# A spectral mixer with its filters: x turned on TensorE and a written-out order, in place of a channels-first copy of x, quarter-tile mixing and a planner

## The chip, the cores and the metric

One core of a Trainium2 chip runs the whole kernel. The metric is the device time of one execution in microseconds, the median of the runs shown.

## What is computed

The input x is 8 images of 128 x 128 positions with 96 channels, all float32. The layer has two halves:

```python
x = x + conv(_ln_c(x), ...)          # normalise over the channels, then the spectral mixer
t = t + ffn(_ln_t(t), ...)           # normalise again, then a quantised MLP 96 -> 384 -> 96

# conv:
x_pre = _soa(jnp.einsum('bhwc,mc->bhwm', x, w1), ...)       # 192 channels, scale * relu^2 + bias
xf = jnp.fft.rfft2(x_pre...)                                # over rows and columns
filt = ... # three small filters, resized to 128 x 65, complex
r = jax.nn.softmax(..., axis=1)                             # three weights per channel, from means over the image
comb = jnp.einsum('shwm,bsm->bhwm', filt, r)
xsp = jnp.fft.irfft2(xf * comb ...)
return jnp.einsum('bhwm,cm->bhwc', xsp, w2)                 # back to 96 channels
```

The MLP's products are of values rounded to fp8 (e5m2), its sums are rounded to float16.

## The kernel before

The Fourier transforms are products with cosine and sine matrices. Every image goes through three streams, which run interleaved: while one image is in the last, the next is in the second and the one after it in the first.

- **Stream a** (`before`, 32 units `u` of four columns of the image): x is read in blocks of 16 columns with rows on the partitions (`load_x`), only to measure mean and variance (`measure`, L581, VectorE). `rstd` makes the reciprocal deviations `ln_r` (ScalarE, VectorE, GpSimd). They go to memory (`store_r`, L650) and come back spread over 96 partitions (`load_r`, L654, tile `rB`). A second copy of x with the channels on the partitions, made by the host, is loaded too (`load_xT`, L646, tile `xT`). `scale` (L659, VectorE) multiplies both into `zT`, 96 x 512, and sums the channels. `project` (L672, TensorE) multiplies by `W1S`, `rectify` (L683) and `square` (L690) are ScalarE, `context` (L697) sums on GpSimd, `transform` (L701, TensorE) is the transform along the rows, `put` (L708, ScalarE) copies it out of PSUM and `store_y` (L711) writes it to the array `Yd`, from ScalarE's DMA queue.
- **Stream s** (`spectrum`, 33 groups `g` of spectrum rows): `load_y` and `load_t` (L842, L848) bring `yt` and the filter rows `tb`; `weigh` (L857) and `pack` (L866) are GpSimd; `along_w` (L874) is the transform along the columns and `filters_of` (L887) the filters' products, in four tiles of 64 x 64 of the array at a time, into `pf`. `make` and `times` (L913, L916, VectorE) multiply the spectra, `turn_back` and `real_basis` (L923, L938, L940, GpSimd) make `xf`. Two groups are then mixed at once by w2: channels 0 to 127 of each half are one product with `w2A` (`mix`, L995), the remaining 64 of each half go in 64 x 64 tiles with `w2B` (`mix_low`, L984), after four products of zeros that open the PSUM banks (L971). `mixed` (L1006) copies out, `invert` (L1011) is the inverse along the columns, `inverted` (L1018) copies out, `store_v` (L1021) writes `Vd`, from ScalarE's queue.
- **Stream c** (`after`, blocks of 16 columns, units of four): `last` (L1123, TensorE) is the inverse along the rows, `residual` (L1131, VectorE) adds x, `measure`, `rstd` and `quantise` (L1151) normalise into fp8 `z`, `turn` (L1156) transposes it by a product with an fp8 identity, `turned` (L1166) copies it out, `first` (L1170), `accumulated` (L1177), `biased` (L1181), `hidden` (L1185), `second` (L1192), `put` (L1203), `bias` (L1207) and `add_up` (L1210) are the MLP, `store` (L1213) writes the result.

**The order.** Nothing is issued where it stands in the code. Each operation is recorded by `at` with a written time: the start and length of its image's stream (`STREAMS`) plus an offset (`O`, for some images `OWN`). Beside the time, an operation carries the operations it needs (`after`), how many PSUM banks it takes and what frees them (`banks`, `until`). `in_order` takes the earliest operation whose needs are placed and for which a bank is free, moves what depends on it back by a lag, and so puts out one order with a bank for each tile. The order of instructions on SyncE, TensorE, VectorE, ScalarE and GpSimd is then fixed (`PINNED`). Six banks serve all products but the filters', which have two of their own (`psz`).

Of the kernel before, what the change touches and what calls it, by code (L numbers as in the profile page):

```python
# [22 lines left out]

# [21 lines left out]
MED = 192  # L45
# [12 lines left out]
NP = 16  # L58
WB = 16
HB = WB // 2  # L60
# [6 lines left out]
    "a": ((-2.3, 125.8), (125.5, 235.3), (361.7, 294.9), (654.8, 258.7), (914.4, 293.7), (1208.1, 250.0), (1549.9, 242.8), (1792.3, 246.3)),  # L67
    "s": ((145.6, 218.8), (374.7, 303.7), (677.8, 243.8), (924.7, 275.3), (1223.3, 298.2), (1520.9, 283.8), (1811.0, 258.1), (2086.7, 264.0)),
    "c": ((456.0, 260.1), (727.0, 260.5), (1018.6, 240.5), (1251.4, 323.7), (1604.0, 246.4), (1857.3, 253.2), (2101.5, 235.3), (2381.7, 138.0)),
# [3 lines left out]
    ("a", 0): {  # L73
        "a_load_xT": -1.97,
        "a_load_r": -5.06,
        "a_store_r": -9.58,
        "a_load_x": -10.466,
        "a_measure": -8.83,
        "a_scale": -1.29,
        "a_project_u0": 0.1,  # L80
        "a_rectify_u0": -4.22,
        "a_project_u2": 0.07,
        "a_rectify_u2": -5.38,
        "a_square": -3.56,
        "a_context": 0.88,
        "a_transform_u0": 1.37,
        "a_put_u0": 1.34,
        "a_transform_u2": 1.21,
        "a_put_u2": -5.7,
        "a_store_y": -2.773,  # L90
        "a_step": 0.26,
        "a_rstd": -4.27,
    },
    ("c", 6): {
        "c_step": 0.17,
        "c_rstd": 5.43,
        "c_quantise": 6.37,
        "c_first": 9.04,
        "c_accumulated": 8.29,
        "c_biased": 7.57,  # L100
        "c_load_v": 0.59,
        "c_last": 1.93,
        "c_residual": 1.66,
        "c_measure": -1.75,
        "c_turn": 8.21,
        "c_turned": 2.68,
        "c_hidden": 10.24,
        "c_second": 11.45,
        "c_put_blkq": 6.6,
        "c_bias": 8.21,  # L110
        "c_add_up": 7.54,
        "c_store": 8.05,
    },
    ("c", 7): {
        "c_step": 0.11,
        "c_rstd": 5.33,
        "c_quantise": 6.22,
        "c_first": 7.65,
        "c_accumulated": 2.03,
        "c_biased": 7.82,  # L120
        "c_load_v": -2.61,
        "c_last": 1.79,
        "c_residual": -0.5,
        "c_measure": -5.02,
        "c_turn": 6.63,
        "c_turned": 6.3,
        "c_hidden": 8.8,
        "c_second": 9.02,
        "c_put_blkq": 9.35,
        "c_bias": 3.04,  # L130
        "c_add_up": 9.99,
        "c_store": 3.47,
    },
    ("s", 7): {
        "s_load_y": -6.85,
        "s_load_t": -3.503,
        "s_weigh": -2.2,
        "s_pack": -2.89,
        "s_along_w_g1": -1.69,
        "s_copy_sr": -3.98,  # L140
        "s_along_w_g0": -5.22,
        "s_filters_of": -1.38,
        "s_make_dmALUsubtract": -2.12,
        "s_make_dpALUadd": -2.45,
        "s_times_t1dm00": -7.26,
        "s_times_t2dp10": -11.08,
        "s_times_t3dm01": -3.94,
        "s_times_t4dp11": -1.04,
        "s_turn_back_g0": -0.01,
        "s_turn_back_g1": -0.53,  # L150
        "s_real_basis_g0": 0.5,
        "s_real_basis_g1": -13.48,
        "s_along_w_g0_x": -1.76,
        "s_alone_z": -4.41,
        "s_filters_of_x": -1.0,
        "s_alone_t": -3.96,
        "s_alone_x": -1.27,
        "s_mix_low": 0.05,
        "s_mix": -0.12,
        "s_mixed": -3.05,  # L160
        "s_invert": 0.88,
        "s_inverted": -2.36,
        "s_store_v": -9.843,
    },
}

T_WEIGHTS, T_CONST, T_ROWS = -112.0, -48.0, (-19.0, 94.0)

O = {
    "a_load_xT": -3.37,  # L170
    "a_load_r": -8.87,
    "a_store_r": -11.4,
    "a_load_x": -10.636,
    "a_measure": -7.71,
    "a_scale": -0.88,
    "a_project_u0": -0.28,
    "a_rectify_u0": -6.09,
    "a_project_u2": 0.13,
    "a_rectify_u2": -4.67,
    "a_square": 0.25,  # L180
    "a_context": 0.82,
    "a_transform_u0": 1.31,
    "a_put_u0": -2.63,
    "a_transform_u2": 1.05,
    "a_put_u2": -2.74,
    "a_store_y": -5.993,
    "s_load_y": -4.81,
    "s_load_t": -2.653,
    "s_weigh": -0.53,
    "s_pack": -0.19,  # L190
    "s_along_w_g1": 0.49,
    "s_copy_sr": -4.8,
    "s_along_w_g0": 0.64,
    "s_filters_of": 0.97,
    "s_make_dmALUsubtract": 0.87,
    "s_make_dpALUadd": 0.85,
    "s_times_t1dm00": -3.01,
    "s_times_t2dp10": -9.29,
    "s_times_t3dm01": -2.33,
    "s_times_t4dp11": 1.37,  # L200
    "s_turn_back_g0": 1.79,
    "s_turn_back_g1": 2.03,
    "s_real_basis_g0": 2.18,
    "s_real_basis_g1": -7.56,
    "s_along_w_g0_x": 0.15,
    "s_alone_z": -4.37,
    "s_filters_of_x": 1.5,
    "s_alone_t": -0.23,
    "s_alone_x": -3.9,
    "s_mix_low": 1.23,  # L210
    "s_mix": 1.38,
    "s_mixed": -0.75,
    "s_invert": 2.22,
    "s_inverted": 0.88,
    "s_store_v": -1.203,
    "a_step": 0.53,
    "a_rstd": -3.83,
    "c_step": 0.22,
    "c_rstd": 4.21,
    "c_quantise": 5.11,  # L220
    "c_first": 6.59,
    "c_accumulated": 5.43,
    "c_biased": 7.0,
    "c_load_v": -2.91,
    "c_last": 0.76,
    "c_residual": -1.01,
    "c_measure": 0.49,
    "c_turn": 6.04,
    "c_turned": 3.07,
    "c_hidden": 7.86,  # L230
    "c_second": 8.37,
    "c_put_blkq": 5.18,
    "c_bias": 3.81,
    "c_add_up": 8.94,
    "c_store": 3.77,
}
BANKS = 6

LAG, TRANSFER_LAG = 0.15, 2.28
PINNED = (  # L240
    mybir.EngineType.SP,
# [26 lines left out]
def _columns(p, r):  # L268

    if p < NP - 1:  # L270
        return [(g, cs) for g in (2 * p, 2 * p + 1) for cs in range(2)]
    return [(NG - 1, 0), (NG - 1, 1)] + [(NG, 0), (NG, 1)] * (r == 0) + [(NG + 1, 0)]


def _constants():
# [14 lines left out]

    turned = []
    for p in range(NP):
        for r in range(2):
            for g, cs in _columns(p, r):
                k = g + 1 + 32 * r if g < NG else 32 if g == NG else 64 * r
                turned.append(k + 64 * cs)
# [4 lines left out]
        "GK": np.concatenate([cos, -sin[1:-1]])[turned] * norm,  # L301
# [18 lines left out]
Op = namedtuple("Op", "time seq what args key needs banks until")  # L320


def in_order(ops):


    keys = {op.key for op in ops}
    assert len(keys) == len(ops)
    left, then, ready, held = {}, defaultdict(list), [], []
    place = {op.key: op.time for op in ops}
    for op in ops:  # L330
        needs = {k for k in op.needs if k in keys}
        left[op.key] = len(needs)
        for k in needs:
            then[k].append(op)
        if not needs:
            heappush(ready, (op.time, op.seq, op))

    free, banks, frees, order = list(range(BANKS)), {}, defaultdict(list), []
    for op in ops:
        for u in op.until:  # L340
            frees[u].append(op)
    pending = {op.key: list(op.until) for op in ops}
    while len(order) < len(ops):
        entry = heappop(ready)
        op = entry[-1]
        if op.banks > len(free):
            held.append(entry)
            continue
        banks[op.key], free = free[: op.banks], free[op.banks :]
        order.append((op, tuple(banks[op.key])))  # L350
        for follower in then[op.key]:
            lag = TRANSFER_LAG if follower.key[1].startswith(("load", "store")) else LAG
            place[follower.key] = max(place[follower.key], place[op.key] + lag)
            left[follower.key] -= 1
            if not left[follower.key]:
                heappush(ready, (place[follower.key], follower.seq, follower))
        for taker in frees[op.key]:

            if len(taker.until) == taker.banks:
                free.append(banks[taker.key][taker.until.index(op.key)])  # L360
            else:
                pending[taker.key].remove(op.key)
                if not pending[taker.key]:
                    free += banks[taker.key]
        while held:
            heappush(ready, held.pop())
    return order


@with_exitstack  # L370
def metaformer_kernel(ctx: ExitStack, tc: tile.TileContext, a: dict, out: bass.AP):
    nc = tc.nc
    x, xT = a["x"], a["xT"]

# [960 lines left out]
```

## Time and profile before

| | before |
|---|---|
| median of 3 runs (lowest to highest) | 2754.84 us (2751.38 to 2756.22) |
| profiled execution: time, span | 2756.22 us, 2754.4 us |
| mean granted TensorE clock | 0.97 |
| DMA | 618.05 MB, 224 GB/s, 480,023 packets |
| largest TensorE lines (recorded) | L672 519 us, L701 431 us, L874 532 us in two groups |
| largest lines of the others | L923 POOL 520 us, L1151 ACT 461 us, L1177 ACT 456 us, L1181 DVE 428 us |

A group of instructions is shown as line, engine, operation, output<-inputs and their sizes, with its busy time and the mean time of one. A float32 product counts as two matmul instructions. A matmul's recorded end is modelled and overlaps the start of the next, so recorded times of a line are longer than what the line takes from its engine; the distance from start to start is the latter. In the slices each digit is the busy share of a fortieth of the span.

### The profile page before, as it was taken

How to read it: one execution, taken by the hardware profiler on the slowest of the kernel's cores; microseconds unless marked ns; L12 is line 12 of the kernel's file. 1: busy time of each engine (PE TensorE's matmuls, PEld its weight loads, DVE VectorE, ACT ScalarE, POOL GpSimd, SP SyncE). 2: the span in 40 equal slices, each digit the busy share in tenths (PEclk: the TensorE clock that was granted, in tenths of full speed). 3: DMA queues.
4: the chain of work that ended last, by engine and by line, in shares of the span. 5: the costliest groups of instructions: out<-in, count | busy, mean ns of one | idle time of the engine just before them, and what ended most of it. 6: DMA issues, size and time to landing. Idle time of an engine off the chain costs nothing.

```text
span 2754.4 us, 69406 instructions
## 1 busy us (share of the span) xinstructions
PE 2567.8 (93%) x25130; PEld 1953.0 (71%) x25130; DVE 2276.1 (83%) x5887; ACT 2233.0 (81%) x4452; POOL 2122.2 (77%) x3246
## 2 busy tenths in 40 slices
PE   4989999999999999999999999999999998999765
PEld 2668877777677777777677777777777776677433
DVE  3557667798898999889898889889889878999786
ACT  2665556699888879889998878889988997888898
POOL 1239997888788878988688969888788886889432
PEclk9899999999999999999999999999999998999896
DMA  7888777977688866878687757888777774656441
GB/s 205 263 263 253 242 224 241 287 233 251 209 255 260 252 213 196 271 242 262 220 258 245 243 171 220 273 259 257 231 239 242 230 222 147 185 178 190 149 129 62
DMA packets 480023, 618.05 MB, mean 224 GB/s; under 512 B 174542, under 2 KB 381270, under 8 KB 479658
## 3 DMA queue, kind: packets, MB, share of 16 engines
q1 hardware_dynamic: 424386, 462.60, 56.8%
q10 hardware_dynamic: 55296, 151.02, 14.7%
q8 instruction: 199, 3.26, 0.5%
q14 instruction: 142, 1.16, 0.1%
HBM read 405.36 MB, written 208.16 MB: 223 GB/s over the span
## 4 chain that ended last, share of the span: by engine, by line
PE 68%; DVE 13%; ACT 7%; POOL 4%; DMA 4%; issue 3%; SPq 1%; POOLq 0%; ACTq 0%; DVEq 0%
PE px L672 13%; PE pz L874 10%; PE py L701 10%; PE pv L995 7%; PE pf L887 6%; PE pg L1011 5%; PE ph L1170 4%; PE pk L1123 4%; PE po L1192 3%; PE pv L984 3%; DVE t L916 3%; DVE y L1181 2%; ACT h L1185 2%; ACT y L1177 2%; DVE st L581 2%
## 5 line engine op out<-in xcount | busy, mean ns | idle before, releaser
L923 POOL TENSOR_TENSOR rr<-t,t 128x390 f32<-128x390 f32 x512 | 520.4, 1017 | 60.4 <-DVE t L916 60.0
L672 PE MATMUL px<-W1S,zT 97*128 97x240 f32 x2048 | 519.4, 379 | 34.1 <-DVE zT L659 29.2
L1177 ACT CAST y<-ph 128x512 f16<-128x512 f32 x768 | 456.0, 603 | 24.2 <-PE ph L1170 22.4
L672 PEld LDWEIGHTS px<-W1S,zT 97*128 97x128 f32 x2048 | 377.2, 194 | 130.0 <-issue 33.7
L1151 ACT ACTIVATE z<-t,ln_m,ln_r 128x96 fp8e5<-128x96 f32 x960 | 461.2, 492 | 8.6 <-POOL ln_m L614 5.7
L1181 DVE TENSOR_SCALAR y<-y,b1q 128x512 f16<-128x512 f16 x768 | 427.5, 568 | 28.2 <-ACT y L1177 25.6
L683 ACT ACTIVATE rl<-px 128x480 f32<-128x480 f32 x512 | 295.7, 581 | 177.5 <-PE px L672 160.2
L701 PE MATMUL py<-X,F 128*128 128x384 f32 x1024 | 430.7, 507 | 2.1 <-ACT X L690 1.9
L1185 ACT ACTIVATE h<-y 128x1536 fp8e5<-128x1536 f16 x256 | 386.2, 1509 | 2.2 <-DVE y L1181 1.6
L659 DVE SCALAR_TENSOR_TENSOR zT<-xT,rB 96x512 f32<-96x512 f32 x256 | 339.8, 1328 | 53.1 <-DMA rB<-Rd 26.5
L874 PEld LDWEIGHTS pz<-F,yt 128*128 128x128 f32 x2080 | 301.4, 192 | 72.0 <-DVE t L1131 5.9
L1210 POOL TENSOR_TENSOR t<-t,o 128x1536 f32<-128x1536 f32 x64 | 210.1, 3282 | 167.8 <-DVE o L1207 165.8
L874 PE MATMUL pz<-F,yt 128*128 128x130 f32 x2080 | 329.0, 281 | 10.2 <-DVE t L1131 4.7
L857 POOL TENSOR_TENSOR tb<-tb,r 128x384 f32<-128x384 f32 (+1 forms) x264 | 287.0, 1087 | 59.7 <-DVE r L808 23.1
L916 DVE TENSOR_TENSOR t<-dm,pf 128x390 f32<-128x390 f32 x512 | 282.6, 552 | 43.8 <-PE pf L887 18.4
L1170 PE MATMUL ph<-zT,W1q 96*128 96x512 fp8e5 x768 | 293.5, 397 | 19.1 <-DVE zT L1166 13.9
L708 ACT COPY yst<-py 128x384 f32<-128x384 f32 x512 | 246.4, 486 | 74.3 <-PE py L701 67.8
L916 DVE TENSOR_TENSOR t<-dp,pf 128x390 f32<-128x390 f32 x512 | 280.3, 548 | 0.0
L940 POOL TENSOR_TENSOR xf<-rr 128x378 f32<-128x378 f32 x256 | 255.3, 997 | 19.7
L995 PEld LDWEIGHTS pv<-w2A,xf 128*128 128x128 f32 x2048 | 246.8, 194 | 13.6 <-issue 1.5
L995 PE MATMUL pv<-w2A,xf 128*128 128x96 f32 x2048 | 255.2, 278 | 0.0
L938 POOL TENSOR_TENSOR xf<-rr 128x390 f32<-128x390 f32 x256 | 250.1, 977 | 0.0
(126 smaller groups left out, 5210.5 us busy)
## 6 DMA issues: line engine op xcount, KB each, us to landing
Yd<-yst ACTq DMA_DIRECT2D x256, 384.0 KB
yt<-Yd SPq DMA_DIRECT2D x256, 384.0 KB
xb<-in_x SPq DMA_DIRECT2D x64, 768.0 KB
xT<-in_xT SPq DMA_DIRECT2D x128, 384.0 KB
rB<-Rd SPq DMA_DIRECT2D x128, 384.0 KB
tb<-T SPq DMA_DIRECT2D x256, 192.0 KB
Vd<-gst ACTq DMA_DIRECT2D x128, 384.0 KB
xr<-in_x SPq DMA_DIRECT2D x64, 768.0 KB
```

Of the source, the lines that this page charges most:

```text
L659: nc.vector.scalar_tensor_tensor(zTs[(b * NU + u) % NZT][:C, :, :], kept["xT", hb][:, :, w].rearrange("c h w -> c w h"), 1.0, kept["rB", h ...
L672: nc.tensor.matmul(px[:, i * (MED + SCTX) : (i + 1) * (MED + SCTX)], lhsT=zTs[(b * NU + u) % NZT][:, i0 + i, :], rhs=W1S, start=True, stop ...
L701: nc.tensor.matmul(py, lhsT=F1, rhs=kept["X", u][:, i0 : i0 + 2, :].rearrange("h w m -> h (w m)"), start=True, stop=True)
L874: nc.tensor.matmul(pz[:, u * 2 * L : (u + 1) * 2 * L], lhsT=y, rhs=F2[:, cs, :], start=True, stop=True)
L916: nc.vector.tensor_tensor(work(name, g), kept[d, g], pair(g, sign, c), ALU.mult)
L923: nc.gpsimd.tensor_tensor(kept["rr", g][:, :, 2 * i : 2 * i + 2, :], kept[ta, g], kept[tb, g][:, :, ::-1, :], op)
L995: nc.tensor.matmul(kept["pv", p, r][:, i * C : (i + 1) * C], lhsT=kept["xf", g][:, cs, r, :], rhs=w2A, start=False, stop=(i == len(_column ...
L1151: nc.scalar.activation(z, t, AF.Identity, bias=m, scale=r, saturate=False)
L1170: nc.tensor.matmul(kept["ph", u, n], lhsT=W1q[:, n * 128 : (n + 1) * 128], rhs=kept["zT", u], start=True, stop=True)
L1177: nc.scalar.copy(kept["y", u][:, n, :], kept.pop(("ph", u, n)))
L1181: nc.vector.tensor_scalar(y, y, b1q[:, n : n + 1], 0.0, ALU.add, ALU.max)
L1185: nc.scalar.activation(kept["h8", u], kept["y", u], AF.Copy, saturate=False)
```

## The change

Stream a no longer has a channels-first copy of x. The x block that was read for measuring is scaled in place, with rows on the partitions (`scale`, VectorE); four transposes a unit (`turn`, TensorE) put it channels first in PSUM, and `turned` (ScalarE) copies it to `zT` and sums it. The round trip of the deviations through memory goes, and with it `xT`, `rB` and `Rd`. The copies of y are stored two units at a time, from SyncE's queue instead of ScalarE's, and so is `Vd`.

Stream s mixes by single groups, not pairs. The quarter tiles and the zeros go: `w2B` is padded with zeros to 128 rows x 192 columns, and the 64 remaining channels of both halves are one product with it, on which the two products with `w2A` add up. `xf` has three buffers instead of four, `xb` three instead of two.

The planner `in_order` goes, with all `after`, `banks` and `until`. The operations are sorted by their written time alone, and the six PSUM banks are taken in turn. SyncE is no longer among the `PINNED` engines. The written times are others: from the third image on each stream takes 335 an image. `filters_of` is the same in both.

```diff
 STREAMS = {
-    "a": ((-2.3, 125.8), (125.5, 235.3), (361.7, 294.9), (654.8, 258.7), (914.4, 293.7), (1208.1, 250.0), (1549.9, 242.8), (1792.3, 246.3)),
-    "s": ((145.6, 218.8), (374.7, 303.7), (677.8, 243.8), (924.7, 275.3), (1223.3, 298.2), (1520.9, 283.8), (1811.0, 258.1), (2086.7, 264.0)),
-    "c": ((456.0, 260.1), (727.0, 260.5), (1018.6, 240.5), (1251.4, 323.7), (1604.0, 246.4), (1857.3, 253.2), (2101.5, 235.3), (2381.7, 138.0)),
+    "a": ((0, 118), (119.0, 243.0), (361.0, 335), (695, 335), (1030, 335), (1365, 335), (1700, 335), (2035, 335)),
+    "s": ((141, 242.1), (412, 335), (747, 335), (1082, 335), (1417, 335), (1752, 335), (2087, 335), (2430, 240)),
+    "c": ((465, 335), (800, 335), (1135, 335), (1470, 335), (1805, 335), (2140, 335), (2475, 240), (2715, 150)),
 }
...
 PINNED = (
-    mybir.EngineType.SP,
     mybir.EngineType.PE,
...
-def in_order(ops):
...
-    stream, free_banks = [None], []
+    events = []
...
-    ps = ctx.enter_context(tc.tile_pool(name="ps", bufs=1, space=PSUM))
+    ps = ctx.enter_context(tc.tile_pool(name="ps", bufs=6, space=PSUM))
...
-    def at(time, what, *args, after=(), banks=0, until=(), name=None):
-        name = name or what.__name__
-        ops.append(Op(time, len(ops), what, args, (stream[0], name) + args, after, banks, until))
+    def at(time, what, *args):
+        events.append((time, len(events), what, args, stream[0]))
...
-        t = ps.tile([128, 512], F32, name=name, tag=f"bank{free_banks.pop(0)}")
+        t = ps.tile([128, 512], F32, name=name, tag="ps")
...
-    w2B = const.tile([128, C], F32, name="w2B")
+    w2B = const.tile([128, 2, C], F32, name="w2B")
...
         def others():
+            nc.gpsimd.memset(w2B, 0.0)
             for i in range(2):
-                nc.sync.dma_start(out=w2B[64 * i : 64 * i + 64, :], in_=a["w2T"][128:, :])
-            make_identity(nc, ident)
+                nc.sync.dma_start(out=w2B[64 * i : 64 * i + 64, i, :], in_=a["w2T"][128:, :])
...
+            xb = pa.tile([128, WB, C], F32, name="xb", tag="xb", bufs=3)
...
-        def load_xT(hb):
-            t = kept["xT", hb] = pa.tile([C, H, HB], F32, name="xT", tag="xT")
-            nc.sync.dma_start(out=t, in_=xT[b, hb, :, :, :])
-
-        def store_r(blk):
-            t = kept["Rd", blk] = dram.tile([2, H, HB], F32, name="Rd", tag="Rd")
-            nc.sync.dma_start(out=t.rearrange("f h w -> h f w"), in_=kept["r", blk].rearrange("h (f w) -> h f w", f=2))
-
-        def load_r(hb):
-            t = kept["rB", hb] = pa.tile([C, H, HB], F32, name="rB", tag="rB")
-            nc.sync.dma_start(out=t, in_=kept["Rd", hb // 2][hb % 2].partition_broadcast(C))
-
-        def scale(u):
-            hb, q = divmod(u, 2)
+        def scale(blk, q):
             w = slice(q * QW, (q + 1) * QW)
-            nc.vector.scalar_tensor_tensor(
-                zTs[(b * NU + u) % NZT][:C, :, :],
-                kept["xT", hb][:, :, w].rearrange("c h w -> c w h"),
-                1.0,
-                kept["rB", hb][:, :, w].rearrange("c h w -> c w h"),
-                ALU.mult,
-                ALU.mult,
+            xb = kept["x", blk]
+            r = kept["r", blk][:, w].unsqueeze(2).to_broadcast([128, QW, C])
+            nc.vector.tensor_tensor(xb[:, w, :], xb[:, w, :], r, ALU.mult)
+
+        def turn(u):
+            blk, q = divmod(u, NQ)
+            pz = kept["pz"] = bank("pzt")
+            for i in range(QW):
+                nc.tensor.transpose(pz[:C, i * 128 : (i + 1) * 128], kept["x", blk][:, q * QW + i, :], ident)
+
+        def turned(u):
+            nc.scalar.activation(
+                zTs[u % NZT][:C, :, :].rearrange("c w h -> c (w h)"),
+                kept["pz"][:C, :],
+                AF.Copy,
                 accum_out=kept["gacc"][:, u : u + 1],
             )
 
         def project(u, i0):
-            px = kept["px", u, i0] = bank("px")[:, : 2 * (MED + SCTX)]
...
         def put(u, i0):
-            if ("yst", u) not in kept:
-                kept["yst", u] = pa.tile([128, QW, MED], F32, name="yst", tag="yst", bufs=3)
-            nc.scalar.copy(kept["yst", u][:, i0 : i0 + 2, :].rearrange("j w m -> j (w m)"), kept.pop(("py", u, i0)))
+            if u % 2 == 0 and i0 == 0:
+                kept["yst"] = pa.tile([128, 2 * QW, MED], F32, name="yst", tag="yst")
+            w0 = u % 2 * QW + i0
+            nc.scalar.copy(kept["yst"][:, w0 : w0 + 2, :].rearrange("j w m -> j (w m)"), kept["py", i0])
 
         def store_y(u):
-            nc.scalar.dma_start(out=Y[b][:, u * QW : (u + 1) * QW, :], in_=kept.pop(("yst", u)))
+            w0 = (u - 1) * QW
+            nc.sync.dma_start(out=Y[b][:, w0 : w0 + 2 * QW, :], in_=kept["yst"])
...
-        def mix_low(p):
...
-                    nc.tensor.matmul(
-                        kept["pv", p, r][half, :n],
-                        lhsT=zeros[rows, :64],
-                        rhs=zeros[rows, :1].to_broadcast([64, n]),
-                        start=True,
-                        stop=False,
-                    )
-            for i in range(5):
-                for h in range(2):
-                    for r in range(2):
-                        if i < len(_columns(p, r)):
-                            g, cs = _columns(p, r)[i]
-                            half, rows = slice(64 * h, 64 * h + 64), slice(64 * r, 64 * r + 64)
-                            nc.tensor.matmul(
-                                kept["pv", p, r][half, i * C : (i + 1) * C],
-                                lhsT=kept["xf", g][rows, cs, 2, half],
-                                rhs=w2B[rows, :],
-                                start=False,
-                                stop=False,
-                            )
...
+        def mix(g):
+
+            xf = kept.pop(("xf", g))
+            pv = kept["pv"] = bank("pv")[:, : 4 * C]
+            for cs in range(2 if g <= NG else 1):
+                o = pv[:, cs * 2 * C : (cs + 1) * 2 * C]
+                nc.tensor.matmul(o, lhsT=xf[:, cs, 2, :], rhs=w2B.rearrange("m n c -> m (n c)"), start=True, stop=False)
+                for u in range(2):
+                    nc.tensor.matmul(
+                        o[:, u * C : (u + 1) * C], lhsT=xf[:, cs, u, :], rhs=w2A, start=False, stop=(u == 1)
+                    )
...
+        def store_v(g):
+            nc.sync.dma_start(
+                out=V[b][:, 4 * (g - 1) : 4 * (g + 1), :],
+                in_=kept["gst"].rearrange("w g (j c) -> w (g j) c", c=C),
             )
             kept_v[b] += 1
 
...
     stream[0] = None
-    at(t - 3 * length / NU - 5, next_pool, after=[(None, "weights")])
-    for op, banks in in_order(ops):
-        free_banks[:] = banks
-        op.what(*op.args)
+    at(t - 3 * length / NU - 5, next_pool)
+    events.sort(key=lambda e: e[:2])
+    for _, _, what, args, _ in events:
+        what(*args)
...
```

## Prediction

> **What bounds the kernel now.** I read the busy shares first, then the slices, then a steady stretch, then the starts inside that stretch.
>
> ```profile
> PE 2567.8 (93%) x25130; PEld 1953.0 (71%) x25130; DVE 2276.1 (83%) x5887; ACT 2233.0 (81%) x4452; POOL 2122.2 (77%) x3246
> PE   4989999999999999999999999999999998999765
> PE 68%; DVE 13%; ACT 7%; POOL 4%; DMA 4%; issue 3%; SPq 1%; POOLq 0%; ACTq 0%; DVEq 0%
> ```
>
> PE is busy nearly everywhere but in the first slices and the last three, and holds two thirds of the chain of waits. The steady stretch, 600 to 2100 us (columns: PE, PEld, DVE, ACT, POOL busy):
>
> ```profile
> 600.00:2100.00 1500.00, 1466.05 (x14727) 1129.97 (x14726) 1328.45 (x3411) 1317.31 (x2666) 1262.67 (x1899) 0.99 0.77 240
> ```
>
> The groups of lines of that stretch count 1208 px matmuls of 256 an image, so 4.72 images pass: **318 us an image**. A matmul's recorded end overlaps its successor, so busy PE overstates; the timeline's start-to-start distances don't:
>
> ```profile
> 1305.69 0.39 PE L1156 MATMUL pz<-ident,z 128*96 128x128 fp8e5 x4
> 1306.01 0.36 PE L971 MATMUL pv<-zeros 64*64 64x384 bf16 x4
> 1306.19 0.83 PE L984 MATMUL pv<-w2B,xf 64*64 64x96 f32 x32
> 1306.95 1.08 PE L672 MATMUL px<-W1S,zT 97*128 97x240 f32 x4
> 1307.87 1.92 PE L995 MATMUL pv<-w2A,xf 128*128 128x96 f32 x16
> 1309.63 0.64 PE L874 MATMUL pz<-F,yt 128*128 128x130 f32 x4
> ```
>
> zeros take 0.18 us from start to next start, the 32 quarter-tile instructions of w2B 0.76, the 16 of w2A 1.76 (1.82 in another set; I use 1.79). Read alike between 1300 and 1345 us: px x4 0.81, py x2 0.65, pz x6 0.67, pf x24 0.83, pg x2 0.70, pk x2 0.66, ph 0.22, po x12 0.51, the fp8 turn x4 0.23 to 0.32 (0.25 taken). Times their numbers in an image: px 64 x 0.81 = 51.8, py 41.6, pz 43.6, pf 27.0, zeros and w2B 15.0, w2A 28.6, pg 22.4, pk 21.1, ph 21.1, po 16.3, turn 8.0, together 296.5 us. So PE really works **93%** of the 318 us; 21.5 us are slack. ACT (1317 us) and DVE (1328) are each at 88% of this stretch, POOL at 84%.
>
> **The skill.** "TensorE: Matmul & The Clock Gate", Terms, gives a transpose mode that is "4× faster for FP32"; no transpose-mode matmul runs in the kernel before, so its trace is silent. The same page, LDWEIGHTS, has a load time go with columns, P/1.2: about 80 ns for 96 and 107 for 128. Here 16 fp32 loads of w2A's 128 columns take 1.96 us, 122 ns each: somewhat more. "Perfetto Trace Analysis", Identifying the Most-Contended Engine, calls matmul busy a bad metric; 1466 busy against some 1395 from starts agrees. "SBUF — State Buffer", SBUF: two separate sides, has a DVE op with two SBUF inputs and a GpSimd op that reads SBUF lock each other out. The scaling at L659 spreads from 985 to 3882 ns (median 1170), which fits.
>
> **Part by part, PE.** Each unit of four columns gains four fp32 transposes (1024 in all), stationary the x tile of 96 columns, moving the 128-column identity. If the mode costs one pass, the nearest row is the fp8 turn of the same shape, 0.23 us per four. If loads don't hide, the row of its loads sets it (0.46 per four):
>
> ```profile
> 1305.46 0.46 PEld L1156 LDWEIGHTS <-z 128*96 128x96 fp8e5 x4
> ```
>
> I take 0.30 per four: 32 x 0.30 = **9.6 us an image** (7.4 to 14.7). If it cost a plain fp32 product, three 130-column pz products in 0.67 us give 0.22 each, and 128 of them 28 us. That is a rival below.
>
> Mixing: per pair of groups 4 zeros, 32 quarter instructions and 16 of w2A go (0.18 + 0.76 + 1.79 = 2.73, x 16 = 43.7 us an image). In come 65 sets of one 192-column and two 96-column fp32 products. By columns a set is 0.32 + 2 x 0.16 = 0.64 us (384 columns take 0.65); by six loads of 122 ns it is 0.73, which I take: 47.5. **+3.8 us** (from -2 to +6, the upper end where the w2A products keep their 0.22). The filters' own 64x64 tiles are the same in both. PE work: 296.5 + 9.6 + 3.8 = **310 us an image**.
>
> **The others.** DVE loses L659 (340 + 20 us for its accumulator reads) and gains 256 products of 128x384; the nearest row, L1131, takes 550 ns, and as both inputs are in SBUF I allow 740: 141 to 190 us. Net -170 to -220, about -25 us an image. It buys nothing while PE sets the period. ACT gains 256 evacuations of 96x512: the fp16 evacuation of 512 columns takes 603 ns, with an accumulator read of DVE's 79 about 0.69, +177 us or 22 an image: 279 + 22 = 301. It stays under PE's 310 but leaves less room. The 384 stores, 326 ns each on ACT's queue, move to SP: up to 15.6 us an image back to ACT's sequencer. POOL: nothing of size, the rows of L923 and L857 stay.
>
> SP loses 128 loads of xT, 128 of rB, 64 stores of Rd and gains 128 merged Y stores and 128 V stores: some 1030 issues at 0.36 us instead of 1100. But a store on SP waits for its copy, and the loads behind it wait too: x, Yd and T loads, and then pack, weigh and PE. Written leads are 11 us (T) to 80 us (x); I price this at zero as long as a store waits less than that, else the order rival applies. DMA loses 100 of 618 MB; at 0.77 busy this is cover, not gain. At the start it saves the Rd round trip (DMA Rd, rB and xT hold 17% of the chain's first 300 us), but the first matmul is at 42.8 us and the next stage is PE work: zero, up to -30.
>
> Order: the planner, which knows what each operation waits for and which bank is free, goes. The new order sorts hand-written times, with six PSUM banks taken in turn; PE is in order, so each wrong place is idle PE. The trace can't show this. Bounds: the planner's 93%, or 85% (a 365 us period). I take 91.5%: 310 / 0.915 = **339 us**.
>
> **Sum.** After: first products near 40 us (before 42.8); stage a of image 0, 51.8 + 41.6 + 9.6 = 103 us of PE, at 95% 108; then a of image 1 with s of image 0, 103 + 140.5 = 243.5, at 95% 256; then the written 104 us until c of image 0 starts: 508, say 510 (before: first pk at 495). Six periods to c of image 6: 2034. The written tail, 2912 - 2475 = 437, stretched by 5% (in the trace the c streams stretch 7.6%: pk from 495 to 2713 where 462 to 2523 is written): 459. Last block and close: 12. Together 3015. The profiled execution's time is 1.8 us above its span of 2754.4, and the median 2754.84 lies between; so the prediction is **3015 us**, +9.4%.
>
> **Rivals.**
> 1. *Hidden, not slower.* The added 13.4 us fit into the 21.5 us of slack, and DVE, 25 us lighter, refills pz and pf banks sooner. Period 318, time 2755. It decides where PE's idle at the changed order can fall below 2.5% of the period. For: L1131 and L913 are rows where DVE and PE wait on each other (DVE dp waited 66 us for pz). Against: 93% is reached with a planner, the new order has none, and ACT gets heavier.
> 2. *Transposes at full fp32 price.* +18.6 us an image: 329 / 0.915 = 359; six periods 120 more and the edges 40: 3175. Against: the skill's mode.
> 3. *The order costs more.* PE at 86%: 360 us, 3015 + 126 + 20 = 3160. For: PE and ACT both near 90% leave little room to absorb misplaced work, and stores block SP.
> 4. *The order costs nothing.* 93%, 333 us, the tail unstretched, the start quicker: 2930.
>
> **Numbers.** Forecast 0.52; rival 4 and a little below it 0.17; rival 3 0.15; rival 2 0.10; rival 1 0.06 (0.03 beyond 0.2% faster, 0.02 within, the rest just slower). 0.2%, 5.5 us, is about what measuring can tell from no change. The range takes in rival 4's value and nearly rival 3's: 2910 to 3155; 0.2 lies outside.
>
> **What would show it.** Right: transposes of 128x128 fp32 in one instruction each, four starting within 0.3 us; px units 335 to 345 us apart per image; PE's slices still 9 from the fourth on; DVE's share near 68%, ACT's near 80%; POOL and DVE idle longer on PE rows. Wrong: 2048 instead of 1024 transpose instructions (rival 2); SP waiting on ACT's yst or gst with PE idle on tb, yt or xb DMAs, or large PE idle behind ACT's PSUM copies (rival 3); a period of 318 (rival 1). The forecast falls if PE's start-to-start work isn't near 310 us an image, or PE's share of the steady stretch isn't 90 to 93%.

## The result, and the profile after

The changed kernel takes **2852.83 us** (2849.47 to 2855.48, four runs) against 2753.11 for the kernel before: ratio 1.0361, 95% interval 1.0343 to 1.0379. It is slower, as forecast, but by 3.6% and not 9.4%; 2853 lies below the range's 2910. The profiled execution took 2855.48 us, its span is 2853.7.

The page of the changed kernel: busy shares, TensorE's slices, the chain of waits by engine.

```profile
PE 2696.3 (94%) x22618; PEld 2109.1 (74%) x22618; DVE 2130.0 (75%) x5630; ACT 2358.3 (83%) x4972; POOL 2024.5 (71%) x3255
PE   6999999999999999999999999999999998988765
PE 78%; DVE 9%; ACT 6%; POOL 3%; issue 2%; DMA 1%; SPq 0%; POOLq 0%; DVEq 0%; ACTq 0%
```

TensorE's busy time is 128 us longer, and its share of the chain rises from 68% to 78%: the changed kernel is more clearly TensorE's than the one before. VectorE lost 146 us, GpSimd 98, ScalarE gained 125. The steady stretch from 600 to 2100 us (columns PE, PEld, DVE, ACT, POOL busy, clock, DMA share, GB/s):

```profile
600.00:2100.00 1500.00, 1491.17 (x12959) 1188.02 (x12958) 1203.44 (x3182) 1350.13 (x2894) 1168.65 (x1864) 1.00 0.60 194
```

The px matmuls of the same stretch, in the kernel before and in the changed one:

```profile
L672 PE MATMUL px<-W1S,zT 97*128 97x240 f32 x1208 | 303.8, 373 | 6.1 <-DVE zT L659 3.3 <-ACT y L1177 1.9 <-ACT gst L1018 0.4
L551 PE MATMUL px<-W1S,zT 97*128 97x240 f32 x1176 | 291.7, 370 | 0.0
```

1176 of 256 an image are 4.59 images: **326.5 us an image**, where the kernel before took 318. One cycle of the timeline of TensorE there:

```profile
1310.22 0.58 PE L811 MATMUL pv<-w2A,xf 128*128 128x96 f32 x4
1310.64 0.52 PE L809 MATMUL pv<-w2B,xf 128*128 128x192 f32 x2
1310.99 0.58 PE L811 MATMUL pv<-w2A,xf 128*128 128x96 f32 x4
1311.41 1.00 PE L551 MATMUL px<-W1S,zT 97*128 97x240 f32 x4
1312.25 0.38 PE L944 MATMUL ph<-zT,W1q 96*128 96x512 fp8e5 x1
1312.47 0.67 PE L966 MATMUL po<-W2q,h 128*128 128x96 fp8e5 x12
1312.98 0.60 PE L538 MATMUL pzt<-ident,xb 128*96 128x128 f32 x4
1313.51 0.90 PE L729 MATMUL pf<-RW,tb 52*64 52x130 f32 x24
```

From start to start, four transposes take 0.53 us here and 0.44 to 0.48 in the cycles after it; the mean over the stretch is 0.46. A set of the padded mixing takes 0.76. With the other rows as before, TensorE's work is 296.5 us, plus 32 x 0.46 = 14.7 for the transposes, plus 65 x 0.76 - 43.7 = 5.7 for the mixing: 317 us an image. So it works **97%** of the 326.5 us, against 93% before. The work grew by 20.5 us an image and the image by 8.6: some 12 us of it fell into time in which TensorE had been idle.

The whole profile can be cut at the first pk product of image 0 and of image 6, as the prediction's sum was:

| us | to c of image 0 | six periods | from there to the end | span |
|---|---|---|---|---|
| before | 495 | 1860 | 400 | 2754 |
| forecast | 510 | 2034 | 471 | 3015 |
| after | 495 | 1941 | 418 | 2854 |

The forecast is 15, 93 and 53 us too long in the three parts.

### The profile page after: what moved, and what is told of

The parts are those of the page before. It is cut to its first block, busy times and chain, and to the rows that moved or that the text cites. A ratio compares the mean times of both kernels' runs of the same rounds, so it can differ in the third digit from the quotient of the medians.

```text
span 2853.7 us, 63672 instructions
## 1 busy us (share of the span) xinstructions
PE 2696.3 (94%) x22618; PEld 2109.1 (74%) x22618; DVE 2130.0 (75%) x5630; ACT 2358.3 (83%) x4972; POOL 2024.5 (71%) x3255
## 4 chain that ended last, share of the span: by engine, by line
PE 78%; DVE 9%; ACT 6%; POOL 3%; issue 2%; DMA 1%; SPq 0%; POOLq 0%; DVEq 0%; ACTq 0%
PE px L551 15%; PE py L576 11%; PE pz L716 10%; PE pv L811 7%; PE pf L729 7%; PE pv L809 6%; PE pg L832 5%; PE ph L944 5%; PE pk L900 4%; PE pzt L538 4%; PE po L966 3%; DVE y L955 2%; DVE t L759 2%; ACT y L951 2%; ACT h L959 2%
## 5 line engine op out<-in xcount | busy, mean ns | idle before, releaser
L955 DVE TENSOR_SCALAR y<-y,b1q 128x512 f16<-128x512 f16 x768 | 417.1, 552 | 255.9 <-ACT y L951 254.0
L551 PEld LDWEIGHTS px<-W1S,zT 97*128 97x128 f32 x2048 | 369.9, 191 | 100.0 <-ACT zT L541 23.9
L959 ACT ACTIVATE h<-y 128x1536 fp8e5<-128x1536 f16 x256 | 381.7, 1491 | 26.8 <-DVE y L955 26.8
L811 PE MATMUL pv<-w2A,xf 128*128 128x96 f32 x2080 | 305.6, 270 | 0.0
L811 PEld LDWEIGHTS pv<-w2A,xf 128*128 128x128 f32 x2080 | 303.4, 193 | 0.0
L984 POOL TENSOR_TENSOR t<-t,o 128x1536 f32<-128x1536 f32 x64 | 198.7, 3105 | 108.1 <-DVE o L981 108.1
L809 PE MATMUL pv<-w2B,xf 128*128 128x192 f32 x1040 | 267.4, 339 | 3.9 <-POOL xf L781 3.7
L779 POOL TENSOR_TENSOR xf<-rr 128x390 f32<-128x390 f32 x256 | 232.2, 907 | 15.8
L729 PE MATMUL pf<-RW,tb 52*64 52x130 f32 x6240 | 239.8, 282 | 1.7 <-POOL rr L766 1.7
```

The source lines that it names most:

```text
L551: nc.tensor.matmul(px[:, i * (MED + SCTX) : (i + 1) * (MED + SCTX)], lhsT=zTs[u % NZT][:, i0 + i, :], rhs=W1S, start=True, stop=True,)
L729: nc.tensor.matmul(pf[64 * h : 64 * h + 64, s, u * 2 * L : (u + 1) * 2 * L], lhsT=tb[p, m0 : m0 + 64], rhs=RW[p, :], start=True, stop=True,)
L809: nc.tensor.matmul(o, lhsT=xf[:, cs, 2, :], rhs=w2B.rearrange("m n c -> m (n c)"), start=True, stop=False)
L811: nc.tensor.matmul(o[:, u * C : (u + 1) * C], lhsT=xf[:, cs, u, :], rhs=w2A, start=False, stop=(u == 1))
L955: nc.vector.tensor_scalar(y, y, b1q[:, n : n + 1], 0.0, ALU.add, ALU.max)
L959: nc.scalar.activation(kept["h8", u], kept["y", u], AF.Copy, saturate=False)
```

## The experiments

All runs are compared with the kernel before on the same chip; the medians of the kernel before were 2750 to 2755 us. Theory P says that TensorE's work sets the time and the written order keeps it at work; what the rivals say stands with each run. The "steady stretch" is always 600 to 2100 us of the run's profile; its px matmuls, 256 an image, give the time of an image.

**1. Without the transposes.** From the changed kernel:

```diff
-                nc.tensor.transpose(pz[:C, i * 128 : (i + 1) * 128], kept["x", blk][:, q * QW + i, :], ident)
...
-                kept["pz"][:C, :],
+                kept["x", blk][:C, :, :].rearrange("c w h -> c (w h)")[:, lo : lo + QW * 128],
```

> The changed kernel (2853 us) without its 1024 transposes on TensorE: ScalarE copies as many elements to zT straight from the x block in SBUF, so the projection works on unturned numbers; ScalarE's and VectorE's work stays. Theory P (TensorE sets the period, and the written order keeps it at work 97% of the time): the four transposes of a unit take 0.44 to 0.54 us from start to next start, 256 units make some 126 us, so 2725 us (2710 to 2755), and the period falls from 326 to about 311. Rival Q (the 97% only mirrors other waits; ScalarE or the order sets the pace): under 40 us come back, 2815 or more.

Measured: 2775.06 us, ratio 1.0068 (1.0043 to 1.0092), 78 us less than the changed kernel. In the profiles the six periods give 67 (1874 instead of 1941), the time to c of image 0 gives 12, the end nothing (417). All 256 units of transposes lie ahead of c of image 6: 75 before c of image 0, 181 in the six periods. At 0.46 us a unit, 35 and 83 us of TensorE's work were gone, so in neither part did all of it come back. In the first part TensorE waited 43 us for zT at the projections, against 4 in the changed kernel. The steady stretch:

```profile
600.00:2100.00 1500.00, 1486.62 (x12805) 1172.67 (x12805) 1249.84 (x3285) 1391.20 (x2994) 1207.67 (x1925) 1.00 0.62 201
```

An image takes 316 us here, and TensorE's work of 302 us is 96% of it. ScalarE (fourth) is now at 93%, but TensorE's recorded idle time in the stretch is only 13 us and the projections have next to none of it (0.3 us), so what keeps the other 16 of the 83 us is not shown. Transposes are the largest single cost, but neither free nor paid in full.

**2. Mixing by pairs in the written order.** `mix_low`, `mix`, `mixed`, `invert`, `inverted` and `GK`'s row order from the kernel before, in the changed kernel:

```diff
-            at(t + o["s_mix"] * P, mix, g)
...
+            at(t + (o["s_mix"] - 0.02) * P, mix_low, p)
+            at(t + o["s_mix"] * P, mix, p)
```

> The changed kernel with the mixing of the kernel before: two groups at once, zeros, quarter tiles of w2B, then w2A; xf with four buffers. P: the padded sets take 0.755 us, 65 of them 49.1 us an image, the pairs 43.7; 5.4 x 8 / 0.97 = 45 us come back, 2808 us (2795 to 2825). Q: no gain, 2845 or more, since two banks at a time and bursts of 48 instructions disturb the regular order.

Measured: 2861.24 us, 1.0382 (1.0362 to 1.0402): Q's value. The six periods do fall, 1941 to 1930, but the end grows from 418 to 437. That the last pair waits for three more columns before c of the last image may load is my reading of this, not a test.

**3. Channels-first x in the written order.** `load_xT`, `store_r`, `load_r` and `scale` of the kernel before replace `scale`, `turn`, `turned`; measuring and `rstd` are written 2.2 units earlier, so that the round trip fits:

```diff
-            at(t + o["a_turn"] * P, turn, u)
-            at(t + o["a_turned"] * P + 0.2, turned, u)
+                at(t + o["a_store_r"] * P, store_r, blk)
...
+                at(t + o["a_load_xT"] * P - 3, load_xT, u // 2)
+                at(t + o["a_load_r"] * P, load_r, u // 2)
```

> The changed kernel with the channels-first x of the kernel before (xT, rB, Rd, scaling at 96x512 on VectorE) in place of the scaling, transposes and copies. P: TensorE loses 126 us of work and the written order still keeps 97%: 2730 us (2710 to 2760). Rival S (the channels-first path itself, with its long VectorE operation and two more loads per half block, is what holds TensorE at 93% in the kernel before): 300.6 / 0.93 = 323 us an image, 2840 us (2800 to 2860).

Measured: 2784.63 us, 1.0105 (1.0080 to 1.0131), 68 less than the changed kernel and halfway between P's value and S's. The six periods are 1882, against 1874 without transposes in run 1. In the steady stretch an image takes 317 us, so TensorE works 95% of it: the channels-first path by itself doesn't hold TensorE at 93%, but P's 97% is not kept either.

**4. Both, so the work of the kernel before in the written order.** Edits 2 and 3, and y stored by single units to make room:

```diff
+            nc.sync.dma_start(out=Y[b][:, u * QW : (u + 1) * QW, :], in_=kept.pop(("yst", u)))
```

> Both together: the products and transfers of the kernel before, in the changed kernel's way of ordering (written times alone, six banks in turn, y and V stored from SyncE, y by single units). P (what the planner loses in TensorE idle is its own): 295.5 / 0.97 = 305 us an image, 2853 - 126 - 45 = 2685 us (2660 to 2720), under both kernels. S: 295.5 / 0.93 = 318 us, about the kernel before, 2755 to 2790.

Measured: 2815.61 us, 1.0221 (1.0197 to 1.0245). P falls, and S is missed in the total. But the steady stretch is what S had put, 318 us an image and 93%, as in the kernel before:

```profile
L577 PE MATMUL px<-W1S,zT 97*128 97x240 f32 x1208 | 301.9, 372 | 5.5 <-ACT yst L613 3.1 <-DVE t L960 2.0
```

So with this work the two orders are equal there. The profile's 57 us beyond the kernel before lie outside: the time to c of image 0 is 483 us, the six periods, which reach past the stretch, are 1892, the end is 437. With padded sets and 5.7 us more work an image (run 3) the six periods are 1882 and the end 415: the padded sets are the cheaper mixing in this order.

**5. Transposes under the planner.** In the kernel before, x is scaled in rows, turned and copied as in the changed kernel, with its needs and bank declared:

```diff
+            at(t + o["a_scale"] * P, scale, u, after=[one("rest", blk), one("measure", blk, q)])
+            at(t + (o["a_scale"] + 0.2) * P, turn, u, after=after, banks=1, until=[one("turned", u)])
+            at(t + (o["a_scale"] + 0.3) * P, turned, u, after=[one("turn", u)] + both("project", u - NZT))
```

> The kernel before with its planner and its mixing by pairs, but x scaled in rows, turned on TensorE and copied by ScalarE as in the changed kernel. TensorE then has the work of the run with pairs in the written order (2861 us). Theory O (the planner's order is worth the 60 us that the two kernels with before's work differ by, 2816 against 2755): 2861 - 60 = 2800 us (2785 to 2825), so the transposes cost 45 under either order. Rival W (transposes cost TensorE's full time in the planner's order, 15.7 us for each of six periods and some 20 in the ramp): 2870 us (2850 to 2890), and then the written order is no worse where there is more TensorE work. Rival H (hidden in the planner's idle): 2755 to 2775.

Measured: 2965.01 us, 1.0772 (1.0747 to 1.0798): worse than every case. The same work in the written order takes 2861. Run 9 gives a reason, the place written for the new steps; with these edits it wasn't tried, so the 1.0772 is no clean price of transposes under the planner.

**6. Padded mixing under the planner.** In the kernel before:

```diff
+            at(t + o["s_mix"] * P, mix, g, after=xf, banks=1, until=[one("mixed", g)])
+            at(t + o["s_mix"] * P + 0.3, mixed, g, after=[one("mix", g)] + empty)
```

> The kernel before with its planner and its channels-first x, but mixing single groups with the padded w2B as in the changed kernel. W: 5.4 us more TensorE work an image, six periods and ramps: +35 to +45, 2795 us. Rival B (as in the written order, where padded sets beat pairs by 8 and 31 us: the bursts of 48 instructions on two banks cost more than their shorter work saves): -8 to -31, 2725 to 2747 us, under both kernels.

Measured: 2785.71 us, 1.0128 (1.0107 to 1.0149), as W has it: 36 us slower. Its six periods are 1875. In the written order the same work took 2784.63, so in the total the two orders are equal with this work.

**7. Both under the planner, so the work of the changed kernel.** Edits 5 and 6:

> The changed kernel's work (transposes and padded mixing) in the planner's order. O: 2853 - 60 = 2793 us (2775 to 2815). W with the padded mixing as dear as its work: 2870 + 40 = 2910 us (2880 to 2930), above the changed kernel. The difference to the run with transposes and pairs under the planner says what the padded mixing is worth beside transposes.

Measured: 3016.73 us, 1.0974 (1.0933 to 1.1016), far above O's 2793 and above W's 2910. Its six periods are 2046. An image of the steady stretch takes 356 us, and TensorE works 89% of it. The projections and their weight loads wait for zT:

```profile
L669 PE MATMUL px<-W1S,zT 97*128 97x240 f32 x1080 | 274.8, 377 | 47.6 <-ACT zT L659 46.8
...
PEld px L669 <- ACT zT L659: 109.0, 109, 3.5
PE px L669 <- ACT zT L659: 76.1, 79, 3.3
```

In the changed kernel the two waits of the whole profile are 24 and 4 us.

**8. The stores on ScalarE's queue.**

```diff
-            nc.sync.dma_start(out=Y[b][:, w0 : w0 + 2 * QW, :], in_=kept["yst"])
+            nc.scalar.dma_start(out=Y[b][:, w0 : w0 + 2 * QW, :], in_=kept["yst"])
```

and V's likewise.

> The changed kernel with the stores of y and V issued from ScalarE's queue again instead of SyncE's. If stores waiting on SyncE hold loads back (SyncE waited 213 us for yst and 99 for gst), 15 us or more come back: under 2840. If the written leads cover it, as the prediction had it: the same within 6 us of 2853; 256 issues of 0.33 us on ScalarE, 83 us in all, could even make it slower by up to 20.

Measured: 2853.89 us, 1.0374 (1.0351 to 1.0396): no difference. Stores that block SyncE cost nothing here, nor do 256 issues on ScalarE.

**9. The planner, with the new steps written earlier.** From run 7:

```diff
-            at(t + o["a_scale"] * P, scale, u, after=[one("rest", blk), one("measure", blk, q)])
+            at(t + (o["a_scale"] - 1.2) * P, scale, u, after=[one("rest", blk), one("measure", blk, q)])
```

and `turn` and `turned` 1.0 and 0.8 of a unit earlier.

> The run with the planner, transposes and padded mixing (3017 us), with scaling, transposes and copies of a unit written about one unit's length earlier (the copy 1.4 us x 8 ahead of where it stood). There the projections waited 76 us on TensorE and 109 at the weight loads for zT. If the planner's loss is the short lead that its new steps were given, 80 us or more come back: under 2940. If it is the planner's order as a whole, under 30: 2990 or more.

Measured: 2882.18 us, 1.0470 (1.0444 to 1.0495): **135 us** less than run 7, for nothing but earlier written times. The wait of px for zT is gone, and an image takes 338 us, of which TensorE works 94%:

```profile
PEld px L669 <- ACT zT L659: 2.1, 4, 0.6
...
L669 PE MATMUL px<-W1S,zT 97*128 97x240 f32 x1136 | 283.3, 371 | 5.9 <-ACT yst L705 2.7 <-ACT y L1145 1.3 <-ACT rl L680 0.8
```

So most of run 7's loss was the lead I had given the new steps. It leaves 29 us between the planner and the written order at the changed kernel's work, now 1960 against 1941 in the six periods. Only this one lead was tried; whether another would close the 29 us is open.

**10. The changed kernel with the other stream table.**

```diff
-    "c": ((465, 335), (800, 335), (1135, 335), (1470, 335), (1805, 335), (2140, 335), (2475, 240), (2715, 150)),
+    "c": ((486.0, 260.1), (757.0, 260.5), (1048.6, 240.5), (1281.4, 323.7), (1634.0, 246.4), (1887.3, 253.2), (2131.5, 235.3), (2411.7, 138.0)),
```

and a and s likewise.

> The changed kernel with the stream table of the kernel before (s begins 20 us and c 30 us later, so that stored y and V are there): lengths of 219 to 324 us, each image's streams in another ratio, in place of 335 for all; offsets, work and the sorting by time stay. Theory R (TensorE reaches 97% since all three streams step at one rate, so that one cycle of about 10 us with the same waits repeats): the six periods lengthen to 93%, 340 us each, 2950 us (2900 to 3000). Rival (the table matters little, the offsets carry it): 2853 to 2880.

Measured: 2947.29 us, 1.0698 (1.0671 to 1.0724), R's value. In the steady stretch an image takes 343 us, and TensorE works 92% of it, about what R says. From c of image 0 to c of image 6 the loss is smaller: of the profile's 96 us only 38 lie there (1979); 32 come before, where the later starts of s and c count, and 26 after. The steady stretch has TensorE's recorded busy time down from 1491 to 1451:

```profile
600.00:2100.00 1500.00, 1450.57 (x12336) 1143.88 (x12333) 1142.03 (x3016) 1287.97 (x2752) 1096.66 (x1770) 0.99 0.57 185
...
L551 PE MATMUL px<-W1S,zT 97*128 97x240 f32 x1120 | 282.6, 374 | 7.6 <-ACT zT L541 4.1 <-ACT y L951 3.1 <-ACT sr L752 0.4
```

So the even table is part of what brings this order to 97% with this work.

**11. The kernel before with an even table.**

```diff
+    "c": ((456.0, 277), (733.0, 277), (1010.0, 277), (1287.0, 277), (1564.0, 277), (1841.0, 277), (2118.0, 238), (2365.0, 138)),
```

and a and s likewise.

> The kernel before with an even stream table: 277 for every image of every stream from the third on (268, 238 and 138 in the last stages), the planner, the offsets and the work unchanged. Theory R (streams that step at one rate leave TensorE less idle, whoever orders them): its six periods, now 310 us of 296.5 us work, fall towards 303, so 2710 to 2735 us, under both kernels. Rival (uneven table and offsets were fitted to each other and to the planner, as the written offsets to their even one): 2755 or more, up to 2850.

Measured: 2795.37 us, 1.0159 (1.0142 to 1.0176). R falls as a general rule: even streams are no gain by themselves, and an image of the steady stretch still takes 318 us. Exchanging the table and keeping the offsets costs 42 us in the one kernel and 94 in the other, as the rival has it for a table and offsets that were fitted to each other.

The ratios to the kernel before, by order and work:

| | xT, pairs | xT, padded | transposes, pairs | transposes, padded |
|---|---|---|---|---|
| planner | 1 | 1.0128 | 1.0772 | 1.0974; 1.0470 with lead |
| written order | 1.0221 | 1.0105 | 1.0382 | **1.0361** |

And the time of an image in the steady stretch, with the share of it that TensorE works (its work is about 296.5, 302, 311 and 317 us from left to right):

| | xT, pairs | xT, padded | transposes, pairs | transposes, padded |
|---|---|---|---|---|
| planner | 318, 93% | 322, 94% | 346, 90% | 356, 89%; 338, 94% with lead |
| written order | 318, 93% | 317, 95% | 324, 96% | **326.5, 97%** |

None of the versions beats the kernel before. The other cells keep the written times of one of the two kernels, with few changes, for work that these were not written for; so a step between cells can also hold the loss of that fit.

## Why the prediction was wrong

**Right: what binds, and which way.** TensorE works 93% of the steady stretch before and 97% after, and holds most of the chain in both; VectorE's relief of 146 us bought nothing that shows; the period rose when TensorE's work did. By the table of ratios, one way from 1 to 1.0361 is padded mixing under the planner (+1.28%), the exchange of the order at that work (nothing: 1.0128 and 1.0105 overlap), transposes for the channels-first path (+2.5%). By the other way, the order comes first (+2.2%), then transposes (+1.6%), then padding (-0.2%, inside the intervals). The parts don't add up independently.

**The step that failed: the order.** I took the planner's 93% for a ceiling ("Bounds: the planner's 93%, or 85%"), and set the written order at 91.5% because it has no planner. It reaches 97%. At the work as it measured, 317 us, 91.5% would have been 346.5 us an image; 326.5 were measured. So the order term was 20 us an image too dear, 120 us in six images. Nothing in the trace before had said that 93% was a ceiling; it was one order's value with one work, and I read a bound into it.

Under this lies a second fault: I divided the work by a share as if the share stayed the same whatever the work. Run 4 has the changed kernel's way of ordering with the work before, and works 93%, no more than the planner. The 20.5 us of added work then lengthen its image by 8.6 us. Under the planner with the longer lead (run 9) the same added work lengthens the image by 20 us, and there the share does stay (94%). Run 10 shows that the even table has a part in the 97%; why the written order takes in more work at so little cost is otherwise not shown.

Run 7, the changed work in the planner's order with an untuned lead, takes 3017 us, next to my 3015. That is luck and no support for the forecast: its image takes 356 us where I had put 339, and its three parts are 564, 2046 and 408 us where I had 510, 2034 and 471. Exchanging its order for the written one is worth 164 us, and run 9 shows that 135 of these are lead time for the new steps and not the planner as such.

**Six images are not six periods.** I took six steady images for the time from c of image 0 to c of image 6. In the kernel before this would have given 6 x 318 = 1908 us, where the table has 1860, and its trace could have told me: its last px starts at 2265 us and c of image 6 at 2354, so at the end of that time stream a has nothing left to do. In the changed kernel six images are 1959 and the measured time is 1941. So the forecast's 2034 becomes 1941 by +45 for the work that I sized too small, -120 for the order and -18 for the missing stream.

**The tail.** I stretched the written 437 us by 5%, as the c streams had stretched in the kernel before, and added 12. It took 418. In the kernel before, the end that is written in the same way, from the start of c of image 6 (2101.5) to the last `add_up` (2558.5), is 457 us and took 400: the streams had stretched, their end had not. These times order operations, they don't measure them.

**Mis-sized terms, the other way.** Transposes: 0.30 us per four, measured 0.44 to 0.53 and 0.46 on average, above the nearest row's 0.23 to 0.32 and at the price of 0.46 for loads that don't hide: 5 us an image too little. Mixing: 0.73 per set, measured 0.76, 2 us. At 91.5% they would have added some 45 us to six images, which hid part of the order's error. The single pass is confirmed: 1024 instructions for 1024 transposes, so rival 2 falls.

**ScalarE.** The copies last 601 ns in the record, as expected, and their accumulator reads 204, not VectorE's 79:

```profile
L541 ACT ACTIVATE zT<-pzt 96x512 f32<-96x512 f32 x256 | 153.9, 601 | 40.6 <-PE pzt L538 39.9
L541 ACT ACTIVATION_READ_ACCUMULATOR zT<-pzt 96x1 f32 x256 | 52.3, 204 | 0.0
```

But the records of ScalarE overlap too, so these durations can't be added up. From start to start (medians) it is 489 ns from a copy to its read and 93 from the read to the next operation: 582 ns, 149 us in all, where I had 0.69 us and 177. The engine's busy time rose by 125, other rows having become a little shorter (z from 492 to 481 ns, h from 1509 to 1491).

**The rest.** SyncE's stores at zero price: right (run 8). The row scaling took 724 ns where 740 was allowed. The start: c of image 0 begins at 495 us in both kernels, although TensorE has about 23 us more work ahead of it. The first product comes 16 us sooner (27 us instead of 43), a gain that I had let go to zero. GpSimd's 98 us less were not foreseen: several of its rows are shorter (L940's from 997 to 939 ns); the reason was not tried.

**The rivals.** Rival 3 (the order costs more) had the wrong sign. Rival 4 (the order costs nothing) came nearest, but with 93% as its best; the kernel went 77 us beyond it. Rival 1's mechanism, added work that goes into slack, is half of what happened: 12 of 20.5 us. It needed TensorE's idle time to fall below 2.5%; it fell to 3%, but TensorE's work grew by 20.5 us and not 13.4.

## What to carry to other kernels

The busy share that an order reaches with one work is no bound for another order, nor for the same order with another work: here the written order stood at 93% and at 97%. So price the work from start-to-start distances, keep a term of both signs for the order, up to the engine's full 100%, and ask how much of the added work the idle time can take in. If a period is to be multiplied, do it for the kernel before first and compare. A new step's lead time can be worth more than the step (135 us here, against 68 to 78 for the transposes), so an operation added to a tuned schedule has to be tried at several leads before its cost is believed.

## What had not been expected of the hardware

Four fp32 transposes of 128 x 96 take 0.44 to 0.53 us from start to start, 0.11 to 0.13 each, where an fp32 product of 130 columns takes 0.22: about half, not the quarter that the Trainium skill, "TensorE: Matmul & The Clock Gate" (Terms), gives for transpose mode. In the steady stretch the median from one transpose to the next is 109 ns for 128 columns; one of the two instructions of a float32 product takes 112 ns for 130 columns (pz), 202 for 240 (px) and 325 for 384 (pk, pg). At 0.84 to 0.85 ns a column, as the last two give, 128 columns are 108 ns. So a transpose costs what one of a product's two instructions costs, and half of the prediction's own 0.22 would have been its price. The weight loads take 0.39 us per four in the same cycle:

```profile
1312.94 0.39 PEld L538 LDWEIGHTS pzt<-ident,xb 128*96 128x96 f32 x4
```

That is somewhat less than the four transposes take, so the loads don't have to set the pace; loads and columns were not tried apart.
